# Toeplitz coefficients stored channel-innermost, and scan inputs in one ring of six with first columns copied three pairs at a time

## The chip, the core and the metric

The program runs on one core of one Trainium2 chip. The metric is device time in microseconds of one execution, as the median of three runs. One further execution was profiled; all rows below come from it.

## What is computed

The reference chains four image blocks on `x` (8 images of 56 x 56 pixels, 192 channels). The second (windowed attention) and the third (a depthwise 3 x 3 convolution) are not touched by the change. The first and the fourth are, and this is what matters of them:

```
# block 1: a gated Toeplitz mix, D1 = 576 channels
decay = concat([one, gamma, one, gamma[:, ::-1]], axis=1)[0]
a1 = _rpe_mlp(rpe_input, ...) * decay          # one coefficient per offset and channel
a2 = _rpe_mlp(rpe_input, ...) * decay
qv = q * v
o1 = _toeplitz(qv along w, a1)                 # per channel a 56 x 56 Toeplitz product
o2 = _toeplitz(qv along h, a2)
out = (p * (o1 + o2)) @ o_w.T + o_b
# block 4: a selective scan, 4 directions, 384 channels, 16 states each
dA  = exp(delta * A);   dBu = (delta * u) * B
hs[t] = dA[t] * hs[t-1] + dBu[t]               # along the 3136 pixels
y = sum over n of hs[n] * C[n],  + D * u
```

All of it is float32.

## The kernel before, in words

**Setting up.** A small network (lines 145 to 184) makes the coefficients: for each axis `i` a tile `ea` of 96 channels x 6 groups x 112 offsets, written by one DMA of GpSimd (L184) to `ext[i]` in DRAM, one row of 112 floats per channel. All its memory comes from a pool `rpe`, whose place the following stage reuses, so the first load of that stage (L195) waits until the last of these DMAs has landed.

**The Toeplitz stage** runs twice, each time on four images: `products` (L187) forms `qv` and stores it, `toeplitz` (L228) multiplies. The first pass (images 0 to 3) runs alone. The second (images 4 to 7, `beside=True`) is interleaved, in program order, with `front(0)`, which prepares image 0 for the scan; no scan starts before it is through. Within a pass there are two axes of six groups of 96 channels, so twelve groups. For one group the queue of SyncE (SP) loads the products in eight DMAs into `tzx` (L251, 56 partitions each), and then, for each block of 24 channels, two DMAs (L259) fill the two diagonal 56 x 56 quarters of `tm`, a tile of 112 partitions x 24 channels x 112 positions. There are three `tm` tiles in turn. The source is an overlapping view of `ext`: partition p reads, for each channel, the 56 floats from offset p on. So one of these DMAs consists of 56 x 24 runs of 56 floats (224 bytes). TensorE then makes one product per channel (L263), with `t[:, c, :]` as the stationary operand and `x[:, :, c]`, whose step is 96 floats, as the moving one. A float32 product is two instructions, so one group is 192 of them. Results are copied back into `x` (L269), and when a group is done GpSimd's queue writes it with eight DMAs (L277).

**The scan stage** goes over 224 chunks (8 images x 4 directions x 7 chunks of 448 pixels). A chunk has 24 pairs: three groups `d` of 128 channels by eight pairs `k` of states; 5376 pairs in all. For pair g the steps are:

- `inject` (L991, GpSimd): `hs` = du x B, 2 x 448 elements, into a tile of a pool of five
- `decay` (L1006, ScalarE): two exponentials into a PSUM tile of a pool of two
- `initial` (L996, ScalarE): the two first values of the states, into the first (or last) column of `hs`
- `scan` (L1015, VectorE), into PSUM or, for k in 1, 4, 6, in place into `hs`
- `times_c` (L1021): times C, on GpSimd for k in 1, 4, 6 and on VectorE for the other five
- `keep_state` (L1028, ScalarE): the last column is saved for the next chunk
- `add_up` (L1036, TensorE): summed over the states by products with the identity.

Per chunk and d, `times_x` (L979, GpSimd) makes `du` = delta x u from a tile `xcd` that SP loads (L969).

**What sets the order.** The loop of this stage (lines 1185 to 1239) is written out by hand and kept as written. At step g it issues `inject(g+2)` and then, if pair g-1 belongs to GpSimd, its `times_c`; on ScalarE `keep_state(g-1)`, the exponentials of g+1 and `initial(g+2)`; then the scan of g. The loads of the next chunk stand at (d, k) = (1, 0), and its three `times_x` at (1, 6), (1, 7) and (2, 0). Between pairs a planner (`Parts`, L1051) inserts pieces of the next image's `front` and of `finish`; it keeps a model clock for each engine, to which every step adds a written-down cost, and lets a piece in where the model has room.

Of the kernel before, what the change touches and what calls it, by code (L numbers as in the profile page):

```python
# [15 lines left out]
F32 = mybir.dt.float32  # L16
# [15 lines left out]
PT_ = WS * 2 * WS  # L32
DI, NS, R = 384, 16, 12
ND = DI // 128
NG = 2
NP = NS // NG
SLAB, SLAB_F = 10048, 2688
# [44 lines left out]
def model(ctx: ExitStack, tc: tile.TileContext, a: dict, out: bass.AP):  # L82
# [13 lines left out]
    nc.vector.memset(eps5, 1e-5)  # L96
    stats0 = const.tile([CP, B, 2, 2], F32, name="stats0")

    ext = [dram.tile([D1, TT], F32, name=f"ext{i}") for i in range(2)]

    qv_d = [dram.tile([D1 // CP, L, CP], F32, name=f"qv{b}") for b in range(B)]
    o_d = [[dram.tile([D1 // CP, L, CP], F32, name=f"o{i}_{b}") for b in range(B)] for i in range(2)]
# [13 lines left out]
    def blocks(ap):  # L116
        return ap.rearrange("(k p) l -> p k l", p=CP)
# [27 lines left out]
    with tc.tile_pool(name="rpe", bufs=2) as rp, tc.tile_pool(name="rpe_ps", bufs=2, space=PSUM) as rps:  # L145
        pos = load_const(rp, "pos")
        slope = load_const(rp, "slope")
        nc.vector.tensor_scalar(slope, slope, 0.0, 1.0, ALU.max, ALU.min)
        nc.vector.tensor_scalar(slope, slope, 1.0 - 0.95, 0.95, ALU.mult, ALU.add)
        zeros = rp.tile([CP, W - 1], F32, name="zeros")  # L150
        nc.vector.memset(zeros, 0.0)

        decay = rp.tile([CP, 6, TT], F32, name="decay")
        nc.vector.memset(decay, 1.0)
        for c in range(6):
            nc.vector.tensor_tensor_scan(
                decay[:, c, W : 2 * W - 1],
                slope[:, c : c + 1].to_broadcast([CP, W - 1]),
                zeros,
                1.0,  # L160
                ALU.mult,
                ALU.add,
            )
            nc.vector.tensor_copy(decay[:, c, 0 : W - 1], decay[:, c, 2 * W - 2 : W - 1 : -1])
        for i in range(2):
            w0, b0 = load_const(rp, f"t{i}_w0"), load_const(rp, f"t{i}_b0")
            ws, bs = load_const(rp, f"t{i}_ws"), load_const(rp, f"t{i}_bs")
            wo, bo = load_const(rp, f"t{i}_wo"), load_const(rp, f"t{i}_bo")
            h = rp.tile([32, TT], F32, name="rpe_h")
            nc.vector.tensor_scalar(h, pos, w0, b0, ALU.mult, ALU.add)  # L170
            nc.vector.tensor_scalar_max(h, h, 0.0)
            for j in range(3):
                ph = rps.tile([128, 512], F32, name="ps_rpe")
                nc.tensor.matmul(ph[:32, :TT], ws[:, j, :], h, start=True, stop=True)
                h = rp.tile([32, TT], F32, name="rpe_h")
                nc.vector.tensor_scalar(h, ph[:32, :TT], bs[:, j : j + 1], 0.0, ALU.add, ALU.max)
            ea = rp.tile([CP, 6, TT], F32, name="rpe_ea")
            for c in range(6):
                pa = rps.tile([128, 512], F32, name="ps_rpe")
                nc.tensor.matmul(pa[:CP, :TT], wo[:, c * CP : (c + 1) * CP], h, start=True, stop=True)  # L180
                nc.vector.scalar_tensor_tensor(
                    ea[:, c, :], pa[:CP, :TT], bo[:, c : c + 1], decay[:, c, :], ALU.add, ALU.mult
                )
            nc.gpsimd.dma_start(out=blocks(ext[i]), in_=ea)  # L184


    def products(images, beside):  # L187
# [38 lines left out]


    def toeplitz(images, beside):  # L228
        TC = 24
        G = len(images) * (H // 2)  # L230
        with (
            tc.tile_pool(name="tz", bufs=2) as sp,
            tc.tile_pool(name="tz_t", bufs=1) as tp,
            tc.tile_pool(name="tz_ps", bufs=4 if beside else 8, space=PSUM) as ps,
        ):

            tm = [tp.tile([TT, TC, TT], F32, name=f"tm{i}") for i in range(3)]
            for t in tm:
                nc.gpsimd.memset(t, 0.0)
            n_t = 0  # L240
            for ax in range(2):
                along_h = "(h u w) c -> u h w c"
                along_w = "(u h w) c -> u w h c"
                stored = "(w u h) c -> u w h c"
                size = dict(h=H, u=2) if ax == 0 else dict(w=W, u=2)
                for c0 in range(D1 // CP):
                    x = sp.tile([TT, G, CP], F32, name="tzx", bufs=2 if beside else 3)
                    for n, b in enumerate(images):
                        v = qv_d[b][c0].rearrange(along_w if ax else along_h, **size)
                        for u in range(2):  # L250
                            nc.sync.dma_start(out=x[u * W : (u + 1) * W, n * 28 : (n + 1) * 28, :], in_=v[u])  # L251
                    for c1 in range(0, CP, TC):
                        t = tm[n_t % 3]
                        n_t += 1
                        e = ext[1 - ax][c0 * CP + c1 : c0 * CP + c1 + TC, :]

                        src = bass.AP(e.tensor, e.offset, [[1, W], [TT, TC], [1, W]])
                        for u in range(2):
                            nc.sync.dma_start(out=t[u * W : (u + 1) * W, :, u * W : (u + 1) * W], in_=src)  # L259
                        for c2 in range(0, TC, 4):  # L260
                            po = ps.tile([TT, 4, G], F32, name="ps_tz")
                            for c in range(4):
                                nc.tensor.matmul(  # L263
                                    po[:, c, :], t[:, c2 + c, :], x[:, :, c1 + c2 + c], start=True, stop=True
                                )
                            cs = slice(c1 + c2, c1 + c2 + 4)
                            copy = nc.vector.tensor_copy if (c2 // 4) % 2 or beside else nc.scalar.copy

                            copy(  # L269
                                x[:, :, cs].rearrange("p (b g) c -> p b g c", g=28)[:, :, ::-1, :],  # L270
                                po.rearrange("p c (b g) -> p b g c", g=28),
                            )
                            yield 1.0
                    for n, b in enumerate(images):
                        v = o_d[ax][b][c0].rearrange(stored if ax else along_h, **size)
                        for u in range(2):
                            nc.gpsimd.dma_start(out=v[1 - u], in_=x[u * W : (u + 1) * W, n * 28 : (n + 1) * 28, :])  # L277
# [8 lines left out]
    with (  # L286
# [9 lines left out]
        Dsum = wp.tile([128, ND], F32, name="Dsum")  # L296
        ones = wp.tile([128, 128], F32, name="ones")
        nc.vector.memset(ones, 1.0 / DI)
        zero2 = wp.tile([128, NG], F32, name="zero2")
        nc.vector.memset(zero2, 0.0)  # L300
        slab = wp.tile([128, SLAB], F32, name="slab")
        slab_f = wp.tile([128, SLAB_F], F32, name="slab_f")

# [661 lines left out]

        def load_xc(i, d):
            b, slot, j = chunks[i]
            t = sp.tile([128, CH], F32, name="xcd", bufs=4)
            nc.sync.dma_start(out=t, in_=xc_d[slot // 2][b][:, d, j * CH : (j + 1) * CH])  # L969
            return t  # L970

# [3 lines left out]
            nc.sync.dma_start(out=delta[:, :, 1 : CH + 1], in_=dl_d[slot][b][:, :, j * CH : (j + 1) * CH])  # L975

        def times_x(i, d):
            du = dus[i, d] = sp.tile([128, 1, CH], F32, name="du", bufs=4)
            nc.gpsimd.tensor_mul(du[:, 0, :], deltas[i][:, d, 1 : CH + 1], xcs.pop((i, d)))  # L979

        def tokens(i):
# [5 lines left out]

        def inject(g):
            i, d, k = pairs[g]
            hs = hss[g] = sp.tile([128, NG, CH + 1], F32, name="hs", bufs=5)  # L990
            nc.gpsimd.tensor_mul(hs[:, :, tokens(i)[0]], dus[i, d].to_broadcast([128, NG, CH]), bms[i, k])  # L991

        def initial(g):
            i, d, k = pairs[g]
            src = zero2 if i % NCH == 0 else states[i - 1][:, d, NG * k : NG * k + NG]
            nc.scalar.copy(hss[g][:, :, tokens(i)[1]], src)  # L996

        def decay(g):
            i, d, k = pairs[g]
# [143 lines left out]
        sp = own.enter_context(tc.tile_pool(name="sc", bufs=2))  # L1143
        bcp = own.enter_context(tc.tile_pool(name="bc", bufs=NP))
        ysum = wp2.tile([128, ND, L], F32, name="ysum")
        delta2 = wp2.tile([128, 2, ND, CH + 2], F32, name="delta2")

        for u in range(2):
# [4 lines left out]
        with tc.manual_schedule():  # L1153
# [11 lines left out]

            def feed(g):
                inject(g)
                fed[g] = run("P", 2.09, taken[g - 5] if g > 4 else 0.0)

            def take(g):  # L1170
                times_c(g)
# [6 lines left out]

            for g in range(ahead):
                feed(g)  # L1180
            initial(0), initial(1)
            prepare(0)
            ahead_of, b_next = None, 1
            ending, anything = None, dict.fromkeys("ADE", 1e9)
            for g, (i, d, k) in enumerate(pairs):
# [5 lines left out]
                if more and d == 1 and k == 0:  # L1191
# [1 line left out]
                    while (b1, slot1 // 2, j1) not in made:  # L1193
                        parts.step(anything, ahead_of)
                    load_delta(i + 1)
                    for e in range(ND):
                        xcs[i + 1, e] = load_xc(i + 1, e)
                if more and (d, k) in ((1, 6), (1, 7), (2, 0)):
                    times_x(i + 1, d + k - 7 if d == 1 else 2)
                    run("P", 1.08)  # L1200
                pi, pd, pk = pairs[g - 1]
                if g + ahead <= last:
# [5 lines left out]
                    run("A", 0.15, scanned[g - 1])  # L1208
                if g < last:
                    prepare(g + 1)  # L1210
                if g + 2 <= last:
                    initial(g + 2)
                    run("A", 0.12, taken[g - 3] if g > 2 else 0.0)
                scan(g)
                scanned[g] = run("D", 2.02, set_[g], fed[g])
                if not on_pool(d, k):
# [132 lines left out]
```

## Time and profile before

| | us |
|---|---|
| median of 3 runs (lowest, highest) | 22281.97 (22275.59, 22308.79) |
| the profiled execution, its own time | 22327.07 |
| its span, first to last instruction | 22325.3 |
| first pass of the Toeplitz products (L263) | from 523.5 |
| second pass | from about 2270 to 3480 |
| scan stage | from 3531 to the end |

The mean granted TensorE clock of the profiled execution is 0.902 of full speed.

| engine | busy us | share of the span |
|---|---|---|
| TensorE | 18177.3 | 81% |
| VectorE | 16627.2 | 74% |
| GpSimd | 16168.9 | 72% |
| ScalarE | 12465.2 | 56% |

In the profile's rows PE is TensorE, PEld its weight loads, DVE is VectorE, ACT ScalarE, POOL GpSimd, SP SyncE; a q behind the name is the queue of that engine. `L263` is line 263 of the kernel. Tiles carry the program's names (`ps_tz<-tzx,tm`: written from the moving `tzx` and the stationary `tm`). A group's row gives its count, the total busy time, the mean of one in ns, and behind the second bar the idle time of the engine just before these instructions, with what ended it.

### The profile page before, as it was taken

The numbers are of one execution on the slowest core, as the hardware profiler recorded it, in microseconds if no ns is written. First come the engines' busy times: TensorE is split into PE (matmuls) and PEld (weight loads), VectorE is DVE, ScalarE is ACT, GpSimd is POOL, SyncE is SP. The second block draws the span as 40 slices with busy tenths as digits, with TensorE's granted clock in tenths as the row PEclk, the third lists the DMA queues.
The fourth block names the chain that finished last, engine by engine and source line by source line (L and its number), as shares of the span: only waits on it lengthen the run. The fifth ranks groups of instructions, "written<-read, shape, count | busy, mean of one in ns | idle before, by whom it ended". The sixth has DMA issues, their size and how long they took to land. (4 is left out here: it accounts for less than half of the span.)

```text
span 22325.3 us, 200421 instructions
## 1 busy us (share of the span) xinstructions
PE 18177.3 (81%) x58372; PEld 9602.0 (43%) x58372; DVE 16627.2 (74%) x13276; ACT 12465.2 (56%) x31719; POOL 16168.9 (72%) x8503
## 2 busy tenths in 40 slices
PE   8668867888887888888888888788888888887666
PEld 4545544434443444344443444344434444343223
DVE  2122216997799768987899779976898789967998
ACT  2116114655666475756665566656565666556555
POOL 0000006987789778987898778977898889878999
PEclk9788878999899989999999989998999999998888
DMA  3941676434544455445544464345544564445333
GB/s 93 203 110 46 162 196 161 134 122 160 178 145 127 143 182 155 124 131 179 172 133 122 156 189 145 125 142 179 152 128 129 177 183 125 125 142 189 127 126 109
DMA packets 2666914, 3250.20 MB, mean 146 GB/s; under 512 B 1175646, under 2 KB 2619072, under 8 KB 2634850
## 3 DMA queue, kind: packets, MB, share of 16 engines
q1 hardware_dynamic: 2645588, 3121.12, 47.2%
q0 software_dynamic: 15520, 116.14, 1.4%
q8 instruction: 463, 7.59, 0.1%
q14 instruction: 639, 5.23, 0.1%
q10 hardware_dynamic: 4704, 0.12, 0.0%
HBM read 2661.35 MB, written 575.48 MB: 145 GB/s over the span
## 5 line engine op out<-in xcount | busy, mean ns | idle before, releaser
L991 POOL TENSOR_TENSOR hs<-du,bm 128x896 f32<-128x896 f32 x5376 | 11093.8, 2088 | 78.7 <-DVE ps_a L1015 49.2
L1036 PE MATMUL ps_y<-hc,ident_sb 128*128 128x448 f32 x21504 | 9838.7, 592 | 746.6 <-POOL hc L1021 670.4
L1015 DVE TENSOR_TENSOR_SCAN ps_a<-ps_a,hs 128x898 f32<-128x898 f32 x3360 | 6796.4, 2023 | 803.8 <-ACT ps_a L1006 564.3
L1006 ACT ACTIVATE ps_a<-delta,A_logs_sb 128x449 f32<-128x449 f32 x10752 | 6859.9, 638 | 357.5 <-DVE hs L1015 75.0
L1036 PEld LDWEIGHTS ps_y<-hc,ident_sb 128*128 128x128 f32 x21504 | 4288.2, 207 | 4813.9 <-issue 3557.6
L1021 POOL TENSOR_TENSOR hc<-hs,cm 128x896 f32<-128x896 f32 x2016 | 4038.6, 2003 | 2127.9 <-DVE hs L1015 992.6
L1021 DVE TENSOR_TENSOR hc<-ps_a,cm 128x896 f32<-128x896 f32 x3360 | 3668.8, 1092 | 1220.5 <-PE ps_y L1036 932.5
L1015 DVE TENSOR_TENSOR_SCAN hs<-ps_a,hs 128x898 f32<-128x898 f32 x2016 | 4064.1, 2016 | 327.7 <-ACT ps_a L1006 241.1
L1028 ACT COPY state<-ps_a 128x2 f32<-128x2 f32 x3359 | 528.1, 157 | 3951.9 <-DVE hc L1021 3949.5
L269 DVE COPY tzx<-ps_tz 112x448 f32<-112x448 f32 x432 | 269.9, 625 | 1551.8 <-PE ps_tz L263 1420.2
L277 POOL DMA_DIRECT2D o<-tzx x192 | 97.3, 513 | 1801.3 <-DVE tzx L269 1797.8
L263 PE MATMUL ps_tz<-tzx,tm 112*112 112x112 f32 x4608 | 905.3, 370 | 585.9 <-DMA tm<-ext 519.0
L263 PEld LDWEIGHTS ps_tz<-tzx,tm 112*112 112x112 f32 x4608 | 880.1, 207 | 629.5 <-issue 625.9
L806 PE MATMUL ps_f<-slab 128*128 128x448 f32 x2646 | 1087.5, 547 | 63.9 <-DMA slab<-dg_d 48.7
L996 ACT COPY hs<-state 128x2 f32<-128x2 f32 x4608 | 817.5, 177 | 2.4 <-POOL hc L1021 2.2
L636 PE MATMUL ps_f<-ident_sb,slab 98*98 98x98 f32 x1344 | 331.0, 314 | 570.5 <-ACT slab L629 570.5
L738 PE MATMUL ps_f<-slab 96*96 96x448 f32 x1764 | 723.6, 546 | 39.5 <-DVE slab L725 39.5
L806 PEld LDWEIGHTS ps_f<-slab 128*128 128x128 f32 x2646 | 507.0, 192 | 563.0 <-issue 509.2
L979 POOL TENSOR_TENSOR du<-delta,xcd 128x448 f32<-128x448 f32 x672 | 707.3, 1053 | 23.3 <-DMA slab<-o 23.2
L76 PE MATMUL ps_f<-slab 96*96 96x448 f32 (+6 forms) x2306 | 694.8, 480 | 25.9 <-DMA slab<-dg_d 22.7
L1028 ACT COPY state<-hs 128x2 f32<-128x2 f32 x2016 | 378.9, 188 | 584.6 <-DVE hs L1015 554.8
L621 ACT ACTIVATE slab<-slab,mxs 98x98 f32<-98x98 f32 x1344 | 489.5, 365 | 370.9 <-DVE mxs L618 370.9
(215 smaller groups left out, 17263.1 us busy)
## 6 DMA issues: line engine op xcount, KB each, us to landing
bm<-bc SPq DMA_DIRECT2D x1792, 448.0 KB
cm<-bc SPq DMA_DIRECT2D x1792, 448.0 KB
xcd<-xc SPq DMA_DIRECT2D x840, 224.0 KB
dl<-slab SPq DMA_DIRECT2D x224, 672.0 KB
delta<-dl SPq DMA_DIRECT2D x224, 672.0 KB
tzx<-qv SPq DMA_DIRECT2D x192, 588.0 KB
o<-tzx POOLq DMA_DIRECT2D x192, 588.0 KB, 13.2
slab<-x SPq DMA_DIRECT2D x224, 336.0 KB
```

The source lines that it names most:

```text
L76: return f(*args, **kw)
L263: nc.tensor.matmul(po[:, c, :], t[:, c2 + c, :], x[:, :, c1 + c2 + c], start=True, stop=True)
L738: nc.tensor.matmul(p[:CP, :CH], dg[:, k, t, :], xp[:, u, k, dy : dy + 8, dx : dx + W], start=t == 0, stop=t == 8,)
L806: nc.tensor.matmul(p[:, :CH], dg[:, t, :], xp[:, 8 * j + dy : 8 * j + dy + 8, dx : dx + W], start=t == 0, stop=t == 8,)
L979: nc.gpsimd.tensor_mul(du[:, 0, :], deltas[i][:, d, 1 : CH + 1], xcs.pop((i, d)))
L991: nc.gpsimd.tensor_mul(hs[:, :, tokens(i)[0]], dus[i, d].to_broadcast([128, NG, CH]), bms[i, k])
L996: nc.scalar.copy(hss[g][:, :, tokens(i)[1]], src)
L1006: nc.scalar.activation(dA[:, n, :], deltas[i][:, d, at : at + CH + 1], AF.Exp, scale=negA[:, slot, d, c : c + 1])
L1015: nc.vector.tensor_tensor_scan(h, dA, hs, 0.0, ALU.mult, ALU.add)
L1021: (nc.gpsimd if on_pool(d, k) else nc.vector).tensor_mul(hc, h[:, :, tokens(i)[0]], cms[i, k])
L1028: nc.scalar.copy(states[i][:, d, NG * k : NG * k + NG], h[:, :, tokens(i)[2]])
L1036: nc.tensor.matmul(yps[i, d][:, :CH], ident, hcs[g][:, n, :], start=k + n == 0, stop=k + n == NP + NG - 2)
```

## The change

1. **Layout of the coefficients.** `ext` becomes 24 blocks of 112 offsets x 24 channels. To write it so, each 96 x 112 piece of `ea` is turned by a product with the identity and copied from PSUM by ScalarE; the DMA then writes runs of 24 floats. `tm` becomes 112 x 112 positions x 24 channels, so the row that partition p reads is one run of 56 x 24 floats (5376 bytes). The stationary operand is now `t[:, :, c]`, with a step of 24 floats.
2. **Ring.** The pool of five `hs` tiles becomes one tile `ring` of six slots, kept apart by their regions. `initial` copies the first values of three pairs at once, at every third step, for the next three pairs.
3. **Smaller pools.** `xcd` and `du` get three buffers instead of four. For this the third `xcd` load moves from (1, 0) to (2, 0), and the third `times_x` from (2, 0) to (2, 6).
4. **The planner's figures** follow: 0.19 for every third step in place of 0.12 for each, and six slots in place of five.

```diff
-    ext = [dram.tile([D1, TT], F32, name=f"ext{i}") for i in range(2)]
+    ext = [dram.tile([D1 // TC, TT, TC], F32, name=f"ext{i}") for i in range(2)]
...
-            nc.gpsimd.dma_start(out=blocks(ext[i]), in_=ea)
+            eT = rp.tile([TT, 6, CP], F32, name="rpe_et")
+            for c in range(6):
+                pt = rps.tile([128, 512], F32, name="ps_rpe")
+                nc.tensor.matmul(pt[:TT, :CP], ea[:, c, :], ident[:CP, :CP], start=True, stop=True)
+                nc.scalar.copy(eT[:, c, :], pt[:TT, :CP])
+            nc.gpsimd.dma_start(
+                out=ext[i].rearrange("n p c -> p n c"), in_=eT.rearrange("p k (n c) -> p (k n) c", c=TC)
+            )
...
-            tm = [tp.tile([TT, TC, TT], F32, name=f"tm{i}") for i in range(3)]
+            tm = [tp.tile([TT, TT, TC], F32, name=f"tm{i}") for i in range(3)]
...
-                        src = bass.AP(e.tensor, e.offset, [[1, W], [TT, TC], [1, W]])
+                        src = bass.AP(e.tensor, e.offset, [[TC, W], [1, W * TC]])
                         for u in range(2):
-                            nc.sync.dma_start(out=t[u * W : (u + 1) * W, :, u * W : (u + 1) * W], in_=src)
+                            dst = t[u * W : (u + 1) * W, u * W : (u + 1) * W, :].rearrange("p i c -> p (i c)")
+                            nc.sync.dma_start(out=dst, in_=src)
...
-                                    po[:, c, :], t[:, c2 + c, :], x[:, :, c1 + c2 + c], start=True, stop=True
+                                    po[:, c, :], t[:, :, c2 + c], x[:, :, c1 + c2 + c], start=True, stop=True
...
-            t = sp.tile([128, CH], F32, name="xcd", bufs=4)
+            t = sp.tile([128, CH], F32, name="xcd", bufs=3)
...
-            du = dus[i, d] = sp.tile([128, 1, CH], F32, name="du", bufs=4)
+            du = dus[i, d] = sp.tile([128, 1, CH], F32, name="du", bufs=3)
...
+        ring = wp2.tile([128, 6, NG, CH + 1], F32, name="ring")
...
-            hs = hss[g] = sp.tile([128, NG, CH + 1], F32, name="hs", bufs=5)
+            hs = hss[g] = ring[:, g % 6]
...
-            src = zero2 if i % NCH == 0 else states[i - 1][:, d, NG * k : NG * k + NG]
-            nc.scalar.copy(hss[g][:, :, tokens(i)[1]], src)
+            at = NG * (NP * d + k)
+            src = zero6 if i % NCH == 0 else states[i - 1].rearrange("p d n -> p (d n)")[:, at : at + 3 * NG]
+            nc.scalar.copy(ring[:, g % 6 : g % 6 + 3, :, tokens(i)[1]], src.rearrange("p (q n) -> p q n", n=NG))
...
-                fed[g] = run("P", 2.09, taken[g - 5] if g > 4 else 0.0)
+                fed[g] = run("P", 2.09, taken[g - 6] if g > 5 else 0.0)
...
-                    for e in range(ND):
+                    for e in range(2):
                         xcs[i + 1, e] = load_xc(i + 1, e)
-                if more and (d, k) in ((1, 6), (1, 7), (2, 0)):
-                    times_x(i + 1, d + k - 7 if d == 1 else 2)
+                if more and (d, k) == (2, 0):
+                    xcs[i + 1, 2] = load_xc(i + 1, 2)
+                if more and (d, k) in ((1, 6), (1, 7), (2, 6)):
+                    times_x(i + 1, k - 6 if d == 1 else 2)
...
-                if g + 2 <= last:
-                    initial(g + 2)
-                    run("A", 0.12, taken[g - 3] if g > 2 else 0.0)
+                if g % 3 == 2 and g < last:
+                    initial(g + 1)
+                    run("A", 0.19, taken[g - 3])
```

More of the change, by code (lines that the diff above doesn't have):

```diff
@@ L34 @@
 ND = DI // 128
+TC = 24
 NG = 2
@@ L228, in toeplitz @@
     def toeplitz(images, beside):
-        TC = 24
         G = len(images) * (H // 2)
@@ L254, in toeplitz @@
                         n_t += 1
-                        e = ext[1 - ax][c0 * CP + c1 : c0 * CP + c1 + TC, :]
-                        src = bass.AP(e.tensor, e.offset, [[1, W], [TT, TC], [1, W]])
+                        e = ext[1 - ax][(c0 * CP + c1) // TC]
+                        src = bass.AP(e.tensor, e.offset, [[TC, W], [1, W * TC]])
                         for u in range(2):
-                            nc.sync.dma_start(out=t[u * W : (u + 1) * W, :, u * W : (u + 1) * W], in_=src)
+                            dst = t[u * W : (u + 1) * W, u * W : (u + 1) * W, :].rearrange("p i c -> p (i c)")
+                            nc.sync.dma_start(out=dst, in_=src)
                         for c2 in range(0, TC, 4):
@@ L298, in model @@
         nc.vector.memset(ones, 1.0 / DI)
-        zero2 = wp.tile([128, NG], F32, name="zero2")
-        nc.vector.memset(zero2, 0.0)
+        zero6 = wp.tile([128, 3 * NG], F32, name="zero6")
+        nc.vector.memset(zero6, 0.0)
         slab = wp.tile([128, SLAB], F32, name="slab")
@@ L1180, in model @@
                 feed(g)
-            initial(0), initial(1)
+            initial(0)
             prepare(0)
```

## Prediction

> **What bounds the kernel now.** I read the busy totals first, then cut the span into stages with the table of engine time by stretch: the first Toeplitz pass, the second, the scan while further images are prepared, and the scan of the last image alone.
>
> ```profile
> core 0: us, PE busy (x) PEld busy (x) DVE busy (x) ACT busy (x) POOL busy (x), PEclk, DMA share, GB/s
> 523.50:1225.00 701.50, 446.73 (x2304) 441.50 (x2304) 89.95 (x144) 76.61 (x144) 44.67 (x89) 0.79 0.88 192
> 2270.00:3480.00 1210.00, 874.39 (x3464) 638.49 (x3462) 222.71 (x369) 187.90 (x244) 53.57 (x96) 0.82 0.70 178
> 3542.00:20258.00 16716.00, 14142.78 (x44643) 7121.71 (x44643) 14073.35 (x10816) 10417.37 (x26948) 14032.67 (x7250) 0.92 0.48 149
> 20258.00:22298.00 2040.00, 1435.60 (x3173) 658.32 (x3171) 1839.18 (x1195) 1148.57 (x2860) 1978.27 (x1026) 0.87 0.41 134
> ```
>
> Three limits show. In the first row the DMA share is 0.88 while PE works 447 of 701 us: transfers bound it. In the second, 0.70 with PE 0.72: mixed. In the third, TensorE, VectorE and GpSimd stand at 0.84 to 0.85 each, ScalarE at 0.62; in the fourth GpSimd is at 0.97. ScalarE, whose copies the change thins out, bounds no stage. The groups that it touches:
>
> ```profile
> L991 POOL TENSOR_TENSOR hs<-du,bm 128x896 f32<-128x896 f32 x5376 | 11093.8, 2088 | 78.7 <-DVE ps_a L1015 49.2
> ...
> L1015 DVE TENSOR_TENSOR_SCAN ps_a<-ps_a,hs 128x898 f32<-128x898 f32 x3360 | 6796.4, 2023 | 803.8 <-ACT ps_a L1006 564.3
> ...
> L263 PE MATMUL ps_tz<-tzx,tm 112*112 112x112 f32 x4608 | 905.3, 370 | 585.9 <-DMA tm<-ext 519.0
> L263 PEld LDWEIGHTS ps_tz<-tzx,tm 112*112 112x112 f32 x4608 | 880.1, 207 | 629.5 <-issue 625.9
> ...
> L996 ACT COPY hs<-state 128x2 f32<-128x2 f32 x4608 | 817.5, 177 | 2.4 <-POOL hc L1021 2.2
> ```
>
> The Toeplitz products lost 519 us to the `tm` loads: 290.7 in the first pass (the view of waits for that stretch) and 228.3 in the second. And from the view of line 1015, what both kinds of scan waited for:
>
> ```profile
>   ACT ps_a L1006: 805.4, 424
>   POOL hs L991: 232.7, 97
> ```
>
> So the scans do wait on ScalarE, 424 times, 1.9 us each. Last, the timeline of two groups late in pass 1, and the DMA view of 620 to 630 us (packets, MB, share of 16 engines):
>
> ```profile
> 1099.40 34.73 SPq L259 DMA_DIRECT2D tm<-ext  x8
> 1100.08 4.05 POOL L277 DMA_DIRECT2D o<-tzx  x8 [59.01 <-DVE tzx L269]
> ...
> 1123.64 37.17 PE L263 MATMUL ps_tz<-tzx,tm 112*112 112x112 f32 x192 [24.76 <-DMA tm<-ext]
> ...
> 1134.48 26.94 SPq L251 DMA_DIRECT2D tzx<-qv  x8
> ```
>
> ```profile
> q0 software_dynamic: 407, 3.38, 85.7%
> q1 hardware_dynamic: 274, 0.06, 3.0%
> ```
>
> A group ends, its outputs leave by GpSimd's queue (q0), and the first `tm` pair of the next group, issued at the same moment on SP's queue (q1), lands only 24 us later. While `o` is written, q1 gets about one packet for each of q0's, but its packets are runs of 224 bytes and q0's of 8.3 KB, so `tm` practically stands.
>
> **Part 1a: the start.** The first load of the following stage (L195) issues at 22.90 us, when the `ext` DMA issued at 19.62 has landed, 3.3 us later. The change puts, ahead of that, six transposes and six ScalarE copies per axis, in three rounds of two PSUM buffers. A round of the like (L180 and L181) takes 1.11 us: 3.3 us. ScalarE's copies alternate, in the built order, with table loads of 1.28 us (the row of ACT_TABLE_LOAD); I count two per axis on the path. Two axes: 2 x (3.3 + 2.6) = 11.8 us. The DMA now has 2688 runs of 96 bytes for 576 of 448; up to 2 us more. Together **+14 us** (6 to 25), on the path: nothing runs beside it.
>
> **Part 1b: `tm` in one run per partition, pass 1.** A pair of DMAs becomes 112 runs of 5376 bytes. Stretches with `o` and long runs of `x` beside each other (2750 to 2766 us) move 328 GB/s, 325 packets of q0 to 303 of q1. A pair beside `o` thus costs 112 x (8.3 + 5.4 KB) / 328 GB/s, about 5 us, where it took 24. By sums per group: `x` 4.82 MB at 204 or 172 GB/s (stretches with `x` alone) takes 23.6 or 28 us; `tm` and `o`, 2.41 + 4.82 MB, at 328 GB/s take 22. That gives a period of 46 to 50 us for the 57 and 62.5 of now (burst 37.2 and gap). The two ends: PE as the bound (37.2 + 5 per group) saves 170 us. At the other, turns aren't packet for packet. [...] If so, small runs would not starve, and only their own rate improves: `tm` alone runs at 153 GB/s (516 to 526 us), 15.7 us per group, and at the 204 GB/s of long runs 11.8, so 4 us x 12 = 45. The trace has 407 runs against 274, near one to one, and the measurement decides. I take 10 us for each of 11 intervals: **-110 us** (-45 to -170).
>
> **Part 1c: pass 2.** Here the loop is interleaved with `front(0)`, and eight `x` loads often stand ahead of `tm` in SP's queue; that part of a wait stays. What shrinks is the pair's own time: 11.5 us where it runs alone (3156.4 to 3167.9), to about 6; and 28 us beside `o` (2750.3 to 2778.8), to some 20 since `x` is still under way. 5 us for each of 12 groups: **-60 us** (-20 to -120).
>
> **Part 1d: strided stationary operand.** Each weight load now reads with a step of 96 bytes. The trace has no strided weight load. It has a strided moving operand: this same matmul, step 384 bytes, starts each 193 to 196 ns (905.3 us / 4608), while L473, with 112 contiguous columns, takes 541.2 / 4704 = 115 ns. [...] Contiguous weight loads of 32, 96 and 128 columns take 109, 164 and 197 ns, about 0.92 ns per column; streaming 112 takes 103 of the 207 ns here. Doubled, 206 ns: 10 more than the slot that hides it. 2304 x 10 ns = 23 us per pass; in pass 1 it goes into the wait for transfers, in pass 2 half does: **+12 us** (0 to 25, if reads of weights and columns don't disturb each other; the other end is the slower rival).
>
> **Part 2: ring and first columns.** Removed: 5376 copies of 177 ns, 952 us. Added: 1792 copies of six elements; the nearest row, state<-hs (L1028), takes 188 ns: 340 us. ScalarE is relieved of 611 us, but only what lies ahead of a late scan counts. In step g it does `keep_state(g-1)`, the exponentials of g+1 and the copy for g+2; the scan of g+1 waits for the exponentials. In 424 waits one copy less stands in front: 424 x 0.177 = 75 us. After every third step the new copy stands between the exponentials and the scan which needs it, where before it was two steps ahead: 141 x 0.19 = 27 back. The copy itself waits for `times_c` of the pair that held its slot, three steps back: the old one did too and lost 2.4 us in all (L996). Behind it on ScalarE stands only the next `keep_state`. The sixth slot removes a part of GpSimd's waits for slots, 49.2 us in 22 (L991, DVE ps_a): 12. **-60 us**. Upper end: ScalarE's backlog is older than one pair, so two copies per wait, 150, and all 49 of the slots, less the 27: -170; lower end: the new copy stands ahead of a scan every third time, 1792 x 0.19 x 0.3 = +100 less 70: +30. In the last image GpSimd is the bound and nothing changes but those slots.
>
> **Part 3: smaller pools.** The third `xcd` load passes, on SP, whatever pieces stand between (1, 0) and (2, 0), and is needed six pairs later, 6 x 3.3 = 20 us, against a landing of a few us. The third `times_x` (1053 ns of GpSimd) moves by six pairs; its count is the same. `du` and `xcd` come free by work of GpSimd itself, earlier. Zero; without the cover a load's 2 to 3 us for each of 223 chunks, 550 us at most.
>
> **Part 4: the planner.** Built, both versions have `front`'s pieces within a few places of each other. Zero, 40 either way.
>
> **Sum.** +14 - 110 - 60 + 12 - 60 = -204. From the profiled 22327.1 us, 22123. That execution was 45 above the median of the runs; less that, 22078: **22080 us**.
>
> **Rivals.**
> *The gap only changes its cause* (0.14). SP's queue is served in order, `x` stands between, and `tm`, early now, waits behind `x`; the scan's copies were hidden as ScalarE's 0.62 suggests. For it: DMA share 0.88, 0.70 in pass 2. Against it: q1 moved 0.06 MB in 10 us. Then -50 + 26 in the Toeplitz part and nothing in the scan: 22258 (22215 to 22300).
> *Weight loads outgrow their slot* (0.10). If strided weights and strided columns are read in turn, a slot is 196 + 103 = 299 ns and a group's burst 57.4 us for 37.2. Pass 1: 12 x 57.4 plus gaps of 6, 761 us, +60; pass 2, 2304 x 106 ns less the 60 above, +184; start +14, scan -60: +198, 22480. It decides where 4608 times the excess, less the 12 x 7 us that pass 1 has free (37.2 + 5 in a period of 49), passes the 216 that the rest saves: 65 ns, so from some 260 ns a slot on. [...]
> *Both ends of the gain* (0.18). Pass 1 to the PE limit, -170; pass 2 -120; scan -170; start and weights +26: 21850 (to 21960).
> The forecast (22080, own range 21960 to 22180) has 0.58.
>
> The range, 21860 to 22300, leaves out the slower rival and half of the deep end. A measurement tells 0.2%, about 45 us, from no change. Faster 0.77, same 0.13, slower 0.10.
>
> **What would show it.** L263's waits for `tm` fall from 290.7 to under 150 and from 228.3 to about 170; gaps of 25 us become about 8; a burst stays at 37.2 to 39 (57 under the rival) with weight loads near 220 ns. The first load after the start issues near 37 us. 1792 copies into `ring` of about 190 ns; the scans' wait on ScalarE falls from 805 to about 740. I am wrong if the burst grows, if PE's gaps persist with `x` as releaser, or if the scan stage moves by over 150 us: then the order of its pieces, which I took as unmoved, did it.

## The result, and the profile after

| | before | changed |
|---|---|---|
| median, us (lowest to highest, 4 runs each) | 22279.9 (22275.59 to 22308.79) | 22079.95 (22056.43 to 22093.29) |
| ratio of times, 95% interval | | 0.9907 (0.9893 to 0.992) |
| the profiled execution's span | 22325.3 | 22054.7 |

The median fell by 200 us, and the number forecast was 22080. That agreement is not worth much: two steps of the sum were wrong, in opposite directions, as the following shows. The two profiled executions differ by 270 us, since that of before lies 45 us above its median and that of after 24 below.

The table of engine time by stretch, for the same four stages of the changed kernel:

```profile
core 0: us, PE busy (x) PEld busy (x) DVE busy (x) ACT busy (x) POOL busy (x), PEclk, DMA share, GB/s
532.50:1110.40 577.90, 510.45 (x2304) 507.82 (x2304) 89.34 (x143) 76.66 (x144) 44.67 (x88) 0.50 0.86 232
2160.00:3388.00 1228.00, 994.07 (x3470) 736.24 (x3468) 223.98 (x370) 189.85 (x249) 55.57 (x99) 0.72 0.64 178
3441.00:19999.00 16558.00, 14087.78 (x44656) 7094.78 (x44655) 14083.94 (x10817) 10119.61 (x23815) 13943.58 (x7249) 0.92 0.49 150
19999.00:22027.00 2028.00, 1449.34 (x3163) 664.74 (x3162) 1838.68 (x1195) 1095.54 (x2411) 1965.58 (x1027) 0.86 0.42 135
```

Pass 1 is 578 us for 701, at 232 GB/s for 192. TensorE, with the same 2304 products, is busy for 510 us instead of 447. Pass 2 has not become shorter: by the starts of its first and last product it takes 1101 us for 1092. The scan of images 0 to 6 is 158 us shorter, that of the last image 12. The groups on the page:

```profile
L1000 POOL TENSOR_TENSOR ring<-du,bm 128x896 f32<-128x896 f32 x5376 | 11104.3, 2092 | 17.3 <-DMA bm<-bc 10.1
...
L1026 DVE TENSOR_TENSOR_SCAN ps_a<-ps_a,ring 128x898 f32<-128x898 f32 x3360 | 6795.9, 2023 | 756.3 <-ACT ps_a L1017 295.2
...
L272 PE MATMUL ps_tz<-tzx,tm 112*112 112x112 f32 x4608 | 1031.7, 404 | 287.2 <-DMA tm<-ext 272.9
L272 PEld LDWEIGHTS ps_tz<-tzx,tm 112*112 112x112 f32 x4608 | 1028.1, 319 | 326.6 <-issue 320.5
```

The waits for `tm` are nearly halved, 519 to 273 us (104 left in pass 1, 169 in pass 2). But a weight load takes 319 ns for 207, and 4608 products take 1032 us for 905. What the two kinds of scan waited for, and the two rows of first-column copies in the view of groups by shape:

```profile
  ACT ps_a L1017: 360.1, 215
  ACT state L1039: 248.3, 124
  ACT ring L1007: 182.2, 92
  POOL ring L1000: 165.4, 117
```

```profile
L1007 ACT COPY ring<-state 128x6 f32<-128x6 f32 x1536 | 283.4, 185 | 0.0
...
L1007 ACT COPY ring<-zero 128x6 f32<-128x6 f32 x256 | 47.2, 184 | 122.1 <-DMA cm<-bc 122.1
```

ScalarE makes 1792 copies of 185 ns, as forecast. Yet the scans still wait for it 431 times and 791 us in all (826 in 433 before): the waits did not become fewer, and another instruction of ScalarE is named as the last. Waits on GpSimd fell by 67 us. The timeline of two groups late in pass 1, and the DMA view of the 6 us from 618 us on, when a group's outputs have just begun to leave:

```profile
1008.42 22.08 SPq L268 DMA_DIRECT2D tm<-ext  x8
...
1012.95 4.05 POOL L286 DMA_DIRECT2D o<-tzx  x8 [46.34 <-DVE tzx L278]
1017.84 42.56 PE L272 MATMUL ps_tz<-tzx,tm 112*112 112x112 f32 x192 [6.09 <-DMA tm<-ext]
1030.85 26.10 SPq L259 DMA_DIRECT2D tzx<-qv  x8
```

```profile
q1 hardware_dynamic: 185, 0.79, 46.8%
q0 software_dynamic: 133, 0.69, 34.8%
```

Beside `o`, SP's queue now moves more than `o` does (0.79 MB in 6 us, where it had moved 0.06 in 10), and TensorE stands for 6 us between groups and not 25. Its burst (the 192 instructions of a group, one behind the other), however, grew from 37.2 to 42.6 us. At the start, the first load of the following stage:

```profile
28.67 1.32 POOL L191 DMA_DIRECT2D ext<-rpe_et  x1 [9.48 <-ACT rpe_et L190]
34.14 0.31 SPq L204 DMA_DIRECT2D wqv<-in_wqv_dram  x1
```

That load stood at 22.90 us: 11.2 us later. The DMA of `ext` lands after 5.5 us where it was 3.3.

### The profile page after: what moved, and what is told of

The parts are those of the page before. It is cut to its first block, busy times and chain, and to the rows that moved or that the text cites. A ratio compares the mean times of both kernels' runs of the same rounds, so it can differ in the third digit from the quotient of the medians.

```text
span 22054.7 us, 196675 instructions
## 1 busy us (share of the span) xinstructions
PE 18328.2 (83%) x58396; PEld 9752.3 (44%) x58396; DVE 16637.5 (75%) x13276; ACT 12126.1 (55%) x28153; POOL 16068.5 (73%) x8503
## 5 line engine op out<-in xcount | busy, mean ns | idle before, releaser
L1000 POOL TENSOR_TENSOR ring<-du,bm 128x896 f32<-128x896 f32 x5376 | 11104.3, 2092 | 17.3 <-DMA bm<-bc 10.1
L1026 DVE TENSOR_TENSOR_SCAN ps_a<-ps_a,ring 128x898 f32<-128x898 f32 x3360 | 6795.9, 2023 | 756.3 <-ACT ps_a L1017 295.2
L1032 POOL TENSOR_TENSOR hc<-ring,cm 128x896 f32<-128x896 f32 x2016 | 3947.5, 1958 | 2086.0 <-DVE ring L1026 991.9
L1032 DVE TENSOR_TENSOR hc<-ps_a,cm 128x896 f32<-128x896 f32 x3360 | 3668.4, 1092 | 1166.5 <-PE ps_y L1047 880.1
L1026 DVE TENSOR_TENSOR_SCAN ring<-ps_a,ring 128x898 f32<-128x898 f32 x2016 | 4063.3, 2016 | 276.6 <-ACT state L1039 121.0
L272 PE MATMUL ps_tz<-tzx,tm 112*112 112x112 f32 x4608 | 1031.7, 404 | 287.2 <-DMA tm<-ext 272.9
L272 PEld LDWEIGHTS ps_tz<-tzx,tm 112*112 112x112 f32 x4608 | 1028.1, 319 | 326.6 <-issue 320.5
L1039 ACT COPY state<-ring 128x2 f32<-128x2 f32 x2016 | 378.7, 188 | 609.7 <-DVE ring L1026 581.0
L482 PE MATMUL ps_f<-ident_sb,slab 112*96 112x112 f32 x4704 | 531.1, 267 | 138.3 <-DVE slab L490 95.0
```

Of the source, the lines that this page charges most:

```text
L272: nc.tensor.matmul(po[:, c, :], t[:, :, c2 + c], x[:, :, c1 + c2 + c], start=True, stop=True)
L482: nc.tensor.matmul(p[:CP, t * TT : (t + 1) * TT], ot[:, n % 2, i, t, c % 2 * CP : c % 2 * CP + CP], ident[:TT, :TT], start=i == 0, stop=i ...
L1026: nc.vector.tensor_tensor_scan(h, dA, hs, 0.0, ALU.mult, ALU.add)
L1032: (nc.gpsimd if on_pool(d, k) else nc.vector).tensor_mul(hc, h[:, :, tokens(i)[0]], cms[i, k])
L1039: nc.scalar.copy(states[i][:, d, NG * k : NG * k + NG], h[:, :, tokens(i)[2]])
```

## The experiments

Ratios are to the kernel before, with 95% intervals, over 4 or 5 runs (14 for `figure`; `strides` and `runs672` ran once, and have none); 0.0010 is 22 us, and a difference of two ratios is known to some 40 us. Lengths of stages are read from the profiles: a pass from its first product's start to its last one's, the scan stage from first to last scan. The kernels whose scan stage is written as in the changed one gave 18586, 18597, 18604, 18612, 18589 and 18624 us, the two with that of before 18756 and 18738: so one profile tells the scan stage to some 20 us. Pass 2 varies by 10 us either way.

**Each half alone.** `layout` has the hunks up to the Toeplitz stage, `ring` the rest.

> Coefficient layout alone (part 1), scan as before. Theory: the parts add, and the layout touches only what lies ahead of the scan: the first scan starts near 3430 us as in the changed kernel (3530.9 before), about -100 us, so near 22180; scan stage 18794 as before. The forecast on record gave this part -144. Rival: the scan stage gains from the layout too (the changed kernel's scan stage is 170 us shorter in its profile), then near 22080 to 22120.

> Ring, thinned copies, smaller pools and planner's figures alone (parts 2 to 4), old layout. Theory: the other half of the gain, -100 us by the medians (22180), with -170 in the scan stage if the profiled run of the changed kernel is typical; the forecast on record gave -60. Rival that the whole is the layout's: 22280.

`layout`: 0.9956 (0.9944 to 0.9969), -98 us; `ring`: 0.9935 (0.9923 to 0.9948), -145. The halves add to -243 where the whole gave -207 (178 to 238), within the intervals. In `layout` the scan stage stays at 18738, in `ring` pass 1 stays at 698 and pass 2 at 1087: neither half works through the other. The forecast had -144 and -60: the first half was overrated, the second underrated.

**The stationary operand's step.** `contig` is the changed kernel with other columns of `tm`, so it computes other numbers:

```diff
-  t[:, :, c2 + c]
+  t.rearrange("p i c -> p (i c)")[:, (c2 + c) * TT : (c2 + c + 1) * TT]
```

> The changed kernel with 112 contiguous columns of tm as the stationary operand in place of 112 columns with a step of 96 bytes (it thus multiplies by other coefficients; transfers, counts and order are the same). Theory, strided weight loads set the slot of 220 ns: slot back to 192 ns, burst of 192 from 42.6 to 37.2 us, weight load from 319 to about 207 ns; pass 1 shorter by 5 x 5 us where PE was the bound and by little where transfers are, pass 2 by up to 64: in all -40 to -90 against the changed kernel. Rival, the granted clock of 0.50 in that pass makes the slot: it stays at 220 while the clock is 0.50. Second rival: transfers and front's pieces take up the room, time as the changed kernel within 20 us.

0.9858 (0.9845 to 0.9871), 109 us faster than the changed kernel. The page's row of the products, and the passes:

```profile
L272 PE MATMUL ps_tz<-tzx,tm 112*112 112x112 f32 x4608 | 907.4, 370 | 359.1 <-DMA tm<-ext 305.4
```

```profile
533.40:1102.30 568.90, 446.17 (x2304) 441.84 (x2304) 89.36 (x143) 76.64 (x144) 44.63 (x88) 0.87 0.89 237
2138.00:3286.00 1148.00, 898.55 (x3507) 651.56 (x3505) 225.87 (x375) 192.04 (x258) 51.48 (x91) 0.85 0.68 189
```

The busy time is that of before, 907 us. Pass 1 gains 9 us of the changed kernel's 577 (16 against the mean of seven kernels with this layout, 585), pass 2 77 of 1101 (71 against their mean, 1095). So the step of 96 bytes costs some 80 us or more, nearly all in pass 2. The granted clock, 0.50 all through pass 1 in the changed kernel, is 0.87 here. The slot (from the start of one product's instruction to that of the next) of 220 ns is not the clock's doing, since in pass 2 of the changed kernel it is 220 both from 2250 to 2350 us, at 0.90, and from 3350 on, at 0.50.

But in pass 2 the slot is not all that changes. Of the groups of TensorE between that pass's first and last product, the two largest of `front(0)`, in the changed kernel and then in `contig`:

```profile
L77 PE MATMUL ps_f<-slab 128*128 128x448 f32 (+2 forms) x661 | 323.8, 639 | 6.4 <-DMA slab<-x 4.1 <-DMA slab<-dg_d 1.6 <-ACT slab L77 0.7
L77 PE MATMUL ps_f<-slab,w_dt_sb 12*128 12x448 f32 x168 | 60.7, 795 | 20.8 <-ACT slab L77 20.8
```

```profile
L77 PE MATMUL ps_f<-slab 128*128 128x448 f32 (+2 forms) x661 | 291.5, 584 | 14.4 <-DMA slab<-x 10.3 <-DMA slab<-dg_d 3.4 <-ACT slab L77 0.7
L77 PE MATMUL ps_f<-slab,w_dt_sb 12*128 12x448 f32 x168 | 52.9, 691 | 17.9 <-ACT slab L77 17.9
```

The granted clock of the pass is 0.70 in the first and 0.83 in the second. Where it is 0.95 or more, the products of `ps_f<-slab` start every 376 ns in the changed kernel, where it is 0.55 or less every 747. So with the step TensorE has 60 us more of Toeplitz products in pass 2 (521 for 461) and 41 us more of `front(0)` (388 for 347, all its products); how the loss divides between slot and clock was not separated.

**Which step costs what.** In `strides`, which ran once and also computes other numbers, the six fours of channels in a block read with different steps of the stationary operand (`ws`) and the moving one (`ms`), in floats:

```diff
-  po[:, c, :], t[:, :, c2 + c], x[:, :, c1 + c2 + c]
+  po[:, c, :], tf[:, w0 : w0 + (TT - 1) * ws + 1 : ws], xf[:, m0 : m0 + (G - 1) * ms + 1 : ms]
+  # (ws, ms) by c2 // 4: (1, 96), (2, 96), (4, 96), (24, 96), (24, 1), (1, 1)
```

> The changed kernel with, for the six fours of channels of each block, these steps (floats) of stationary and of moving operand: (1, 96), (2, 96), (4, 96), (24, 96), (24, 1), (1, 1); it multiplies by other numbers, the counts are the same. [...] Rival A, any step costs: step 2 gives 220 as well. Rival B, the two strided reads disturb each other: (24, 1) is well under 220.

The slots inside a four, medians of 336 each in the first pass, are 192, 192, 198, 220, 220 and 187 ns. The moving operand's step costs 5 ns or nothing; the stationary operand's costs nothing at 8 bytes, 6 ns at 16 and 28 at 96. Both rivals fall: step 2 gives 192 as step 1 does, and (24, 1) gives the 220 of (24, 96). Nor is a moving operand with a step twice as dear, as the prediction read from L473: with both contiguous the slot is 187. The slot here follows the step of the stationary operand; the 115 ns of L473 in the kernel before come from something other than its contiguous columns, and no run shows from what.

**What thinning the copies does.** `perpair` has the ring of six and the smaller pools, but a copy for each pair, two steps ahead, and the planner's old 0.12:

```diff
-  nc.scalar.copy(ring[:, g % 6 : g % 6 + 3, :, tokens(i)[1]], src.rearrange("p (q n) -> p q n", n=NG))
+  nc.scalar.copy(hss[g][:, :, tokens(i)[1]], src)
...
-  if g % 3 == 2 and g < last:
-      initial(g + 1)
-      run("A", 0.19, taken[g - 3])
+  if g + 2 <= last:
+      initial(g + 2)
+      run("A", 0.12, taken[g - 4] if g > 3 else 0.0)
```

> The changed kernel with the first columns copied for each pair again, two steps ahead, from the ring of six; 0.12 per step in the planner. Theory, the thinned copies bring the scan's gain: 60 to 100 us slower than the changed kernel, the scans' wait for ScalarE back near 800 us. Rival, the sixth slot and the smaller pools bring it: within 30 us of the changed kernel.

0.9958 (0.9944 to 0.9972): all of the second half's gain is gone, as in `layout` (0.9956). The ring's sixth slot and the smaller pools, with the order of pieces that goes with them here, are worth nothing. The sixth slot does remove waits (GpSimd's 49 us for slots that a scan held fall to none; 27 us for `keep_state` appear), but the scans' waits on ScalarE are back at 873 us.

**Planner or ScalarE.** `planner` is the changed kernel with the planner told the old costs; `pad` is the changed kernel with ScalarE's time put back.

```diff
-  fed[g] = run("P", 2.09, taken[g - 6] if g > 5 else 0.0)              # planner
+  fed[g] = run("P", 2.09, taken[g - 5] if g > 4 else 0.0)
...
   if g % 3 == 2 and g < last:
       initial(g + 1)
-      run("A", 0.19, taken[g - 3])                                     # planner
+  if g + 2 <= last:
+      run("A", 0.12, taken[g - 3] if g > 2 else 0.0)
...
+  if g % 3 != 2 and g + 2 <= last:                                     # pad, after initial
+      nc.scalar.copy(pad, zero6[:, :NG])
```

> The changed kernel with the planner told the old costs (0.12 on ScalarE at every step, slots of five), instructions otherwise as changed. Theory, it is ScalarE's real time that the thinned copies give back: within 30 us of the changed kernel (0.9907 of before). Rival, the lower figures let the planner place pieces of front elsewhere and that makes the scan stage shorter: 100 us or more of the scan's gain is lost, near 22200.

> The changed kernel with one copy of 128 x 2 into an unused tile put back on ScalarE in each step that has no first-column copy (3584 copies of some 177 ns, about 634 us of ScalarE; nothing waits for them). Theory, what counts is ScalarE's time ahead of late exponentials: 130 to 160 us slower than the changed kernel, the scan stage back at about 18740. Rival, what counts is which scan waits for which copy and when slots come free: within 30 us of the changed kernel.

`planner`: 0.9940 (0.9927 to 0.9952), 74 us slower than the changed kernel with the same instructions, scan stage 18714. `pad`: 0.9909 (0.9894 to 0.9924), no slower, with this row:

```profile
L1230 ACT COPY pad<-zero 128x2 f32<-128x2 f32 x3583 | 628.8, 175 | 0.0
```

```profile
  ACT ps_a L1018: 399.5, 233
  ACT ring L1008: 189.7, 88
  ACT pad L1230: 145.7, 76
  POOL ring L1001: 142.7, 105
  ACT state L1040: 117.3, 50
```

The scans wait 852 us on ScalarE again, more than before the change, and the median does not move. The waits put down to `pad` are not for that copy: 72 of the 76 scans start 101 to 103 ns after the end of their own second exponential, as nearly all of those put down to `ps_a` do (86 to 103). The profiled scan stage, 18640, is 38 us above the mean of the six; at most about that much is ScalarE's time. So the theory, that ScalarE's time ahead of late exponentials is what the change gave back, falls.

**Figure without thinning.** `figure` is the kernel before with one number changed; `perpair_fig` is `perpair` with the same number; `figure0` is the changed kernel with 0.

```diff
-  run("A", 0.12, ...)
+  run("A", 0.19 / 3, ...)      # figure, perpair_fig
...
-  run("A", 0.19, taken[g - 3])
+  run("A", 0.0, taken[g - 3])  # figure0
```

> The kernel before with one number changed: the planner counts 0.063 for a first-column copy (a third of 0.19) in place of 0.12; every instruction is as before, in another order. Theory, the order of front's pieces is what shortens the scan stage: 60 to 130 us faster than before (near 22200). Rival, the figure helps only with the ring of six under it: within 45 us of before.

> The kernel with first columns copied for each pair from the ring of six, now with 0.063 per step in the planner in place of 0.12. Theory, planner's order and not the thinning: as the changed kernel (0.9907 of before) within 30 us, scan stage near 18600, though ScalarE makes all 5376 copies. Rival, thinning has a part of its own: 40 to 75 us slower than the changed kernel.

> The changed kernel with 0 in place of 0.19 for the first-column copy in the planner. Theory, a lower figure lets pieces in earlier and the last quarter of each image is shorter: a further 20 to 80 us. Rival, the gain is one particular order's and not monotone in the figure: no gain, or a loss of up to 100 us.

`figure`: 0.9984 (0.9977 to 0.9992), -36 us with not one instruction changed. `perpair_fig`: 0.9938 (0.9925 to 0.9950), 44 us less than `perpair` and 69 more than the changed kernel. `figure0`: 0.9889 (0.9874 to 0.9904), 40 us below the changed kernel by the middle values, with intervals that overlap: not told apart.

**The order of the pieces, read from the traces.** For each piece of `front` and `finish` one can count the pairs issued before it on its engine, and so compare two kernels place by place. `before` and `layout` have one and the same order, `planner` and `perpair` another, and the changed kernel, `ring` and `pad` a third; within each set not one of 8330 pieces on ScalarE, 3283 on VectorE and 26362 on TensorE differs by a place. That makes a table of two by two, of scan stages (and ratios):

| order of the pieces | a copy or its time for each pair | thinned |
|---|---|---|
| of `planner` and `perpair` | `perpair` 18747 (0.9958) | `planner` 18714 (0.9940) |
| of the changed kernel | `pad` 18640 (0.9909) | 18602, mean of six (0.9907) |

By the scan stage the changed kernel's order is worth 107 us without thinning and 112 with it, and thinning 33 us in the first order and 38 in the second. By the ratios the order is worth 109 and 74 us, and thinning 40 and 4, not told from nothing. The gain of the order stands in the last quarter of each image: 3.97 us per pair in the changed kernel, 3.98 in `ring` and 3.99 in `pad`, but 4.07 in `planner`, 4.08 in `perpair` and 4.07 before. `perpair_fig`, with the lower figure, has a fourth order (44% of ScalarE's pieces lie 1 to 10 pairs from where the changed kernel has them); so it does not test the changed kernel's order without thinning, and its scan stage, 18733, is that of `perpair` within the spread.

**How long a run has to be.** `runs672` is the changed kernel with each `tm` transfer in pieces of 672 bytes:

```diff
-  nc.sync.dma_start(out=dst, in_=src)
+  dst = dst.rearrange("p (q o r) -> p q o r", o=2, r=7 * TC)
+  for o in range(2):
+      part = bass.AP(e.tensor, e.offset + o * 7 * TC, [[TC, W], [2 * 7 * TC, 4], [1, 7 * TC]])
+      nc.sync.dma_start(out=dst[:, :, o, :], in_=part)
```

> The changed kernel with each tm transfer in runs of 672 bytes (8 per partition, by four transfers of a pair in place of two) in place of one run of 5376. Theory, turns packet for packet beside the writing of o: 896 runs of a pair beside the 580 packets of o land some 16 to 18 us after the group's end, so the waits for the first tm of a group rise from 3 to 9 us to about 13 to 16 and pass 1 from 577 to 630 to 680 us. Rival, only the bytes and the own rate of a run count: pass 1 stays under 600 us.

The one run took 22155 us. Pass 1 took 632 us, at the near edge of what the theory of turns gave and above the 600 of the rival. Two groups of it:

```profile
626.56 42.77 PE L275 MATMUL ps_tz<-tzx,tm 112*112 112x112 f32 x192 [4.74 <-DMA tm<-ext]
683.65 42.56 PE L275 MATMUL ps_tz<-tzx,tm 112*112 112x112 f32 x192 [14.32 <-DMA tm<-ext]
```

One wait is of the size that was worked out, most are of 4 to 7 us, one of 25 us near the end has no counterpart in the changed kernel, and new ones arise inside groups, after the first block. So the length of a run matters in steps (224, 672 and 5376 bytes: 698, 632 and 585 us), but the sum of turns is too hard on the middle one. SP also issued twice as many transfers here, and that was not separated.

**A version with contiguous operands.** `best` turns each `tm` block on VectorE into `tn`, of 24 x 112 contiguous floats, one block ahead of use, with loads two blocks ahead, and makes the start's transposed copies on VectorE:

```diff
+  nc.vector.tensor_copy(tn[m % 2], tm[m % 3].rearrange("p i c -> p c i"))
-  po[:, c, :], t[:, :, c2 + c], x[:, :, c1 + c2 + c]
+  po[:, c, :], t[:, c2 + c, :], x[:, :, c1 + c2 + c]      # t = tn[m % 2]
...
-  nc.scalar.copy(eT[:, c, :], pt[:TT, :CP])
+  nc.vector.tensor_copy(eT[:, c, :], pt[:TT, :CP])
```

> The changed kernel with VectorE turning each tm block (112 x 2688, 48 copies per pass) into 24 contiguous 112-column operands, one block ahead, loads two blocks ahead; the start's transposed copies on VectorE in place of ScalarE. Theory: the slot returns to 192 ns as with contiguous columns (0.9858 of before), the start loses its table loads (first load at 29 us in place of 34), the copies of 3 to 6 us lie beside TensorE: 70 to 110 us faster than the changed kernel. Rival, VectorE waits for the transfers in front of its evacuations and TensorE runs out of PSUM: no faster than the changed kernel.

0.9893 (0.9879 to 0.9906): 31 us below the changed kernel by the middle values, with overlapping intervals. The copies cost

```profile
L263 DVE COPY tn<-tm 112x2688 f32<-112x2688 f32 x96 | 336.2, 3503 | 42.4 <-DMA tm<-ext 42.3
```

and the burst is 37.2 us again. Pass 2 falls to 1067, but pass 1 rises to 600: the products wait 5 to 29 us between groups. The profile names no releaser for most of these waits; that they are for a copy whose transfer stands two blocks further ahead, beside `x`, is argued. The start gains 3 us (first load at 31.1 for 34.1). So it beats the kernel before clearly and the changed one by no more than the spread; the 109 us of contiguous columns are only partly to be had this way.

## Why the prediction was right, and where it was not

**Bound by stage.** Right: pass 1 was bound by transfers (TensorE busy for 447 of 701 us, DMA share 0.88), and one run of 5376 bytes in place of 24 of 224 paid there, with 113 us.

**1a, the start, +14.** Right: 11.2 us. Three table loads per axis came, two of them on the path, and the DMA landed 2.2 us later.

**1b, pass 1, -110.** Right: -113 (698 as the mean of three kernels with the old layout, 585 of seven with the new). The low end, 45 us, was the author's estimate for turns that are not packet for packet, under which runs of 224 bytes do not starve; no run shows such turns. What the traces have is 407 packets of `o` beside 274 of `tm` in 10 us, with 0.06 MB moved for `tm`, and two and a half times that low end saved; by what rule the queues take turns was not shown. The other end, 170 us, comes out of its own figures (12 x 42.2 us for 701) as 195. The size came out right with a burst of 42.6 and not the 37 to 39 forecast, since most of the longer burst went into the wait for transfers: `contig` gains only 16 us here.

**1c, pass 2, -60.** Right by itself: with contiguous operands pass 2 is 1025 us for 1092, -67.

**1d, the strided stationary operand, +12.** Wrong: by `contig` it costs 16 in pass 1 and 71 in pass 2, +87 in all, 109 by the medians. Two steps failed. The duration: the sum doubled the 103 ns estimated for the streaming of 112 columns (from loads of 109, 164 and 197 ns for 32, 96 and 128), set these 206 ns against the slot and left out the other 104 ns of the load. The load's row grew by 112 ns (207 to 319), near the doubling, where loads "near 220 ns" were forecast, and the slot by 28 (192 to 220) where 10 were; and that a step doubles a moving operand, read from L473, is not so: it costs 5 ns or nothing. The share: half was to show in pass 2. There 2304 x 28 ns = 65 us of slots came and pass 2 lost 71, but it also lost granted clock (0.70 for 0.83), which made `front(0)`'s products 41 us longer and stood in no term of the sum. So pass 2, forecast at -48 in sum, came out at +4. For the size, `strides` decides: nothing at 8 bytes, 6 ns at 16, 28 at 96; by what mechanism a step costs was not shown.

**2, thinned copies and sixth slot, -60; 4, the planner, zero.** Wrong in size and in mechanism: this half gave -145. The step that failed is the planner's: "Built, both versions have `front`'s pieces within a few places of each other. Zero, 40 either way." The pieces did stay near: two thirds of ScalarE's stand at the same pair in both kernels, the others up to 8 pairs away. What failed is the step from there to zero: by the table of two by two the order is worth about 110 us of scan stage. The other failed term is "one copy less stands in front: 424 x 0.177 = 75": the waits on ScalarE fell by 35 us, not 48, and the thinning is worth 33 to 38 us of scan stage, which the medians do not tell from nothing. VectorE's other waits do not give the cause: those on GpSimd's `inject` fell by 67 us and those on TensorE's `add_up` by 52 (932 to 880), but in `perpair`, which gains nothing, they fell as far (by 74 and 57).

**3, smaller pools, zero.** Nothing in `perpair` speaks against it: its scan stage equals that of before.

In sum: layout -98 for -144, scan -145 for -60. The errors of about +50 and -85 left a total within 40 us, by luck. Two of the signs that the prediction named for being wrong came: the burst grew, and the scan stage moved by 170 us, for which it named the order of the pieces in advance. The rival of weight loads that outgrow their slot was right in kind, at 28 ns over and not 106, but not in its reason, that weights and columns are read in turn: with the moving operand contiguous the slot is 220 ns as well (`strides`).

**What stays open.** Why this order is shorter: no run moved single pieces. It is not simply that pieces stand earlier. In `figure` ScalarE's stand 5 pairs earlier on average than before, for 36 us; in the changed kernel 1 pair later, for some 110 of scan stage; in `planner` and `perpair` nearly 4 later, for next to nothing. Of six orders two gave a short scan stage (18602, and 18608 in `figure0`), four a long one (18714 to 18756), so the good one may be luck of the planner. The thinning's own 33 to 38 us rest on two pairs of profiles, each known to 20, and the copies of `pad` wait for nothing, unlike those of `perpair`. Open too is how pass 2's loss divides between slot and clock.

## What to carry to other kernels

Runs of 224 bytes all but stood here beside packets of 8.3 KB of another queue (0.06 MB moved beside 3.38 in 10 us): lengthen the runs of the queue that is waited for, and look at both queues' packets in the stretch of the wait before choosing. When a layout is turned for the sake of a transfer, look at what TensorE then reads as its stationary operand: the step of the moving operand was nearly free here, that of the stationary one cost 28 ns on a slot of 192, 16 us in the pass that waits for transfers and 71 in the one where TensorE is shared. In a loop whose order a model writes, a changed cost figure is a change of its own; measure it with all instructions kept, and check in the traces which kernels have the same order, before crediting the instructions.

## What the runs showed of the hardware that was not expected

The granted clock stayed at 0.50 through the whole of pass 1 in the changed kernel and in `layout`, where the stationary operand has its step of 96 bytes (TensorE busy 510 of 578 and 583 us), through bursts of 42.6 us without a gap; it was 0.87 with contiguous columns in the same pass (446 of 569 us in `contig`), and 0.84 in `best`, which multiplies by the right coefficients (446 of 599). The busy share alone does not make the difference, since the scan stage has 0.85 at a clock of 0.92; what does was not separated. With the step the slot was 220 ns at 0.50 and at 0.90 alike. ScalarE's PSUM copies at the start drew three table loads of 1.28 us per axis, one after every second copy; with the same copies on VectorE (`best`) the first load of the next stage issued at 31.1 us for 34.1.
